# Four graph-attention layers on one core: layer 0 by lists for half of its targets, and masks stored beside the features

## Chip, core and metric

The kernel runs on one core of a Trainium2 chip. TensorE multiplies, VectorE (DVE), ScalarE (ACT) and GpSimd (POOL) compute beside it, and DMA queues of SyncE (SP), ACT and POOL move data between HBM and the on-chip memory. The metric is the time of one execution on the device in microseconds, as the median of several runs.

## What is computed

Four layers of graph attention over 4096 nodes with 256 features. The adjacency is random, and its density falls with the node number, for targets and sources alike: node 0 has most neighbours, node 4095 fewest.

```python
h = relu(layernorm(x))                 # before every layer
# layers 0, 1: g = h @ W; s = g @ a1, t = g @ a2
e = leaky_relu(s[:, None] + t[None, :], 0.2)
p = softmax(where(adj > 0, e, -big), axis=1)
x = x + p @ g                          # layer 0
x = x + elu(p @ g)                     # layer 1
# layer 2: four heads of 64 features, joined; x = x + joined
# layer 3: two softmaxes, of e and of -e, each times a wide projection; x = x + elu(...)
```

## The kernel before

**Tiles.** The 4096 nodes are 32 tiles of 128 (`NT`), or eight blocks of four tiles (`IB` = 512 nodes). Sources are also taken in chunks of four tiles (`CH`); adjT, the transposed adjacency, is read as 64 chunks of 512 sources by 512 targets in int32 (1 MB, two raw tiles of 512 KB each), turned into bytes on VectorE (L1226), and written to HBM as `mask_t`, one tensor per block.

**Weights of the attention.** The exponential of a leaky ReLU is rewritten so that one VectorE instruction, `weigh` (L963), makes the weights of a source tile against one target tile (128x128) or a whole block (128x512): a maximum of a target row and a per-source scalar, times the mask. TensorE multiplies them with the source's features and a column of ones (L999, 128x257; in layer 2 L1024), accumulating over sources in PSUM.

**Two ways to treat targets.** A *dense* unit handles a block of four target tiles against all 32 source tiles: 32 steps of four matmuls. A *listed* unit handles one target tile. The first four source tiles (`DP` = 4), which are dense in the adjacency, are taken from the on-chip memory (`pre`, masks in `mpre`). Of all other sources only those with an edge into the tile are used: their row numbers stand in `idx`, up to 128 in a column, `CAPS[T]` columns for tile T (from 12 for tile 4 down to 6 for the last eight; 218 columns for tiles 4 to 31). For each column an indirect DMA on POOL fetches 128 rows of features from the layer's `table` in HBM (L1320), and the masks of those rows stand in `mlist`, fetched once for all layers by another indirect DMA (L858).

**Stages.** Layer 0 is dense for all eight blocks, and its features `g0` stay on chip. While it runs, `list_sources` makes the lists of blocks 1 to 7: VectorE and TensorE turn the columns of seen edges into positions, build one-hot matrices (`first`, L839, one buffer of 128 x 128 x 28) and multiply them out (L845), then POOL fetches the masks (L858). Layers 1 to 3 are dense for block 0 and listed for tiles 4 to 31, the dense steps (source order 0, 1, 2, ...) spread between the listed tiles.

**Order of the work.** Python generators stand in two queues, `posts` (ends of tiles and rows of the next layer, `node_rows`: layer norm, transpose L691, projection L713, table write L701 on SP) and `lists_q` (lists). `run` walks through a plan of steps and, after each, takes some of the queued work (`rates`). A step is fetched six places ahead of its matmuls, weighed three ahead (`LEAD`). From that program order a scheduler then sets the order of each engine's instructions, POOL's too. The weights of layers 2 and 3 are loaded on ACT's queue and multiplied out between layers 0 and 1, and the rows of the bias are added to x on POOL (L681).

**Buffers.** Four raw tiles, eight weight tiles (`s_work`), nine gathered tiles of features, six PSUM banks for accumulators and two for all else.

Of the kernel before, what the change touches and what calls it, by code (L numbers as in the profile page):

```python
# [451 lines left out]

DP = CH
JT = NT - DP
TS0 = IT
CAPS = (25, 17, 15, 13, 12, 11, 11, 10, 10, 9, 9, 9, 8, 8, 8, 8) + (8,) + (7,) * 7 + (6,) * 8
# [6 lines left out]
GW = tuple(h * p for h, p in zip(LH, PART))  # L463
LEAD = (0, 2, 3, 6)
# [3 lines left out]
def list_layers(ctx: ExitStack, tc: tile.TileContext, a: dict, out: bass.AP, flag):  # L468
# [5 lines left out]
    work = ctx.enter_context(tc.tile_pool(name="s_work", bufs=8))  # L474
# [32 lines left out]
    mask_t = [dram.tile([N + 1, IB], U8, name=f"mask_t{b}", tag=f"mask_t{b}") for b in range(NIB)]  # L507
    table = [None] + [dram.tile([N + 1, GW[l]], F32, name=f"table{l}", tag=f"table{l}") for l in (1, 2, 3)]

    def table_rows(t, jt):  # L510

        r0 = jt // CH * CH * P
        r0 += 1 if r0 >= HALF else 0
        return t[r0 : r0 + CH * P, :].rearrange("(p k) d -> p k d", k=CH)

# [5 lines left out]
    def weights(l, pool, prep, q):  # L521
# [14 lines left out]
        next(L.making)  # L536
# [121 lines left out]
    def node_rows(L, T0):  # L658
# [16 lines left out]
        for k, T in enumerate(tiles):  # L675
            z = rows.tile([P, D], F32, name=f"s_z_{u}_{k}", tag="z", bufs=4)
            nc.vector.tensor_scalar(z, x[:, T, :], mv[:, k, 0:1], 0.0, op0=ALU.subtract, op1=ALU.max)  # L677
            zs.append(z)
# [18 lines left out]
        for k, T in enumerate(tiles):  # L697
            g = L.rows(T)
            yield from project(L, T, g, hTs[k], r[:, 2, k : k + 1])
            if L.table is not None:  # L700
                nc.sync.dma_start(table_rows(L.table, T)[:, T % CH, :], g)  # L701
            L.ready[T] = True

# [48 lines left out]
    def list_constants(pool):  # L752

        place = pool.tile([P, P, JT], F16, name="place")
        nc.gpsimd.iota(
            place, pattern=[[1, P], [0, JT]], base=0, channel_multiplier=0, allow_small_or_imprecise_dtypes=True
# [27 lines left out]
    def list_sources(ib, seen, pool, consts):  # L784

        n = JT * IT
        place, lists, code, sums = consts
        used = pool.tile([P, JT, IT], F16, name=f"used_{ib}", tag="used")
        nc.vector.tensor_scalar(used, seen, 0.0, None, op0=ALU.is_gt)
        yield  # L790
# [43 lines left out]
        yield  # L834
        for t in range(IT):
            T = ib * IT + t
            cap = CAPS[T]
            first = pool.tile([P, P, JT], F16, name=f"first_{T}", tag="first")
            nc.vector.tensor_tensor(  # L839
                first, place, lof[:, t, :].unsqueeze(1).to_broadcast([P, P, JT]), op=ALU.is_equal  # L840
            )
            ps = ps_mm.tile([P, MAXCAP], F32, name=f"idx_ps_{T}", tag="mm")
            yield
            for j in range(JT):
                nc.tensor.matmul(  # L845
                    ps[:, 0:cap],
                    lhsT=first[:, :, j],
# [9 lines left out]
            for k in range(cap):  # L857
# [3 lines left out]
                    in_=mask_t[ib],  # L861
                    in_offset=bass.IndirectOffsetOnAxis(ap=idx[:, k : k + 1], axis=0),
                    element_offset=t * P,
                )
            yield

    index = {}
# [16 lines left out]
    def target_rows(L, T0, nt, big, nact):  # L884
# [3 lines left out]
        grow = (L.big if big else rows).tile(  # L888
            [P, L.H, w], F32, name=f"s_grow_{L.l}_{T0}", tag="growb" if big else "grow"
# [21 lines left out]
    class Unit:  # L911
# [4 lines left out]
        def __init__(u, L, T0, nt, n, get, big=False, heads=None, like=None, cost=1.7, nact=0, rates=(2, 1), per=1):  # L916
# [65 lines left out]
        def multiply(u, i):  # L982
            L, n = u.L, u.L.part - 1
            heads, g, p = u.steps.pop(i)
            first, last = i < u.per, i >= u.n - u.per
# [136 lines left out]
    def run(plan):  # L1122

        n = len(plan)
        for p in range(n + LEAD[3]):
# [5 lines left out]
            if p >= LEAD[3]:  # L1131
# [3 lines left out]
                pump(lists_q, u.rates[1])  # L1135


    with ExitStack() as phase:
# [4 lines left out]
        gpool = phase.enter_context(tc.tile_pool(name="s_g0", bufs=1))  # L1143

# [9 lines left out]
        def zero_rows():  # L1154
# [3 lines left out]
            for b in range(NIB):  # L1158
                nc.sync.dma_start(mask_t[b][HALF : HALF + 1, :], zero[:, 0 : IB // 4].bitcast(U8))
            for l in (1, 2, 3):  # L1160
                for k in range(0, GW[l], D + 2):
                    n = min(D + 2, GW[l] - k)
# [3 lines left out]
        g0 = gpool.tile([P, NT, GW[0]], F32, name="g0")  # L1166
        L0.rows = lambda T: g0[:, T, :]

        def rows_of(L):
            def f(T):  # L1170
                if T < DP:
                    return L.pre[:, T, :]
                return rows.tile([P, GW[L.l]], F32, name=f"s_g_{L.l}_{T}", tag="gout", bufs=3)

            return f

        half = CH // 2

        loaded = {}

        def load(n):

            ib, c = divmod(n, NCH)
            loaded[n] = []
            for h in range(2):
# [8 lines left out]
                loaded[n].append(raw)  # L1194

        def behind(c):
# [5 lines left out]
            if c == 5:  # L1202
                L1 = weights(1, const, prep, nc.sync)
                L1.pre = keep.tile([P, DP, GW[1]], F32, name="pre1")
                L1.rows = rows_of(L1)
                push(posts, L1.making)

        def block(ib):
            masks = {}
            seen = lists_p.tile([P, JT, IT], F32, name=f"seen_{ib}", tag="seen", bufs=2)  # L1210

            def get(jt):
                if jt % CH == 0:
                    c = jt // CH
                    n = ib * NCH + c
                    if n + 1 < NIB * NCH:
                        load(n + 1)
                    if ib == 0:
                        behind(c)
                    m = (  # L1220
                        mpre[:, :, ib * IB : (ib + 1) * IB]
                        if c == 0
                        else mpool.tile([P, CH, IB], U8, name=f"s_m_{ib}_{c}", tag="m")
                    )
                    for h, raw in enumerate(loaded.pop(n)):
# [195 lines left out]
```

## Time and profile before

| | us |
|---|---|
| median of 3 runs (1837.76 to 1842.36) | 1838.87 |
| the profiled execution | 1842.63 |
| its span, first to last instruction | 1840.9 |

| engine | busy us | share of the span |
|---|---|---|
| TensorE matmuls (PE) | 1751.7 | 95% |
| TensorE weight loads (PEld, overlapping) | 1479.2 | 80% |
| VectorE | 1362.7 | 74% |
| POOL | 990.1 | 54% |
| ACT | 607.2 | 33% |

A float32 matmul appears as two records of each kind. Spans on POOL are rough. A share of busy time is an average over four layers that wait for different things, so the stretches have to be read one by one.

### The profile page before, as it was taken

The numbers are of one execution on the slowest core, as the hardware profiler recorded it, in microseconds if no ns is written. First come the engines' busy times: TensorE is split into PE (matmuls) and PEld (weight loads), VectorE is DVE, ScalarE is ACT, GpSimd is POOL, SyncE is SP. The second block draws the span as 40 slices with busy tenths as digits, with TensorE's granted clock in tenths as the row PEclk, the third lists the DMA queues.
The fourth block names the chain that finished last, engine by engine and source line by source line (L and its number), as shares of the span: only waits on it lengthen the run. The fifth ranks groups of instructions, "written<-read, shape, count | busy, mean of one in ns | idle before, by whom it ended". The sixth has DMA issues, their size and how long they took to land.

```text
span 1840.9 us, 29987 instructions
## 1 busy us (share of the span) xinstructions
PE 1751.7 (95%) x9818; PEld 1479.2 (80%) x9818; DVE 1362.7 (74%) x3899; ACT 607.2 (33%) x1793; POOL 990.1 (54%) x950
## 2 busy tenths in 40 slices
PE   6999999999998888988899999999999999999997
PEld 5888888888887666766647777779999888888886
DVE  7766887887884445676689888989888466677775
ACT  5620110110010001233227766769997101111111
POOL 4200677644733767777735555355563477565551
PEclk9999999999999699998999999999999999999999
DMA  7644646635622334454423233333332567656652
GB/s 257 235 154 143 196 121 182 208 108 176 214 58 63 79 108 134 133 152 123 117 66 104 75 93 106 82 91 103 104 94 76 158 204 210 194 171 184 185 153 88
DMA packets 128434, 253.30 MB, mean 138 GB/s; under 512 B 21857, under 2 KB 50958, under 8 KB 128270
## 3 DMA queue, kind: packets, MB, share of 16 engines
q0 software_dynamic: 45344, 119.48, 24.9%
q1 hardware_dynamic: 79690, 129.96, 21.2%
q10 hardware_dynamic: 3236, 1.84, 0.4%
q8 instruction: 81, 1.33, 0.3%
q14 instruction: 83, 0.68, 0.1%
HBM read 215.32 MB, written 35.89 MB: 136 GB/s over the span
## 4 chain that ended last, share of the span: by engine, by line
PE 86%; DVE 5%; DMA 4%; issue 2%; ACT 1%; POOL 1%; ACTq 0%; DVEq 0%; POOLq 0%
PE s_acc L999 51%; PE s_accm L1024 21%; PE s_pj L713 7%; DMA s_gg<-table,idx 4%; PE idx_ps L845 3%; DVE s_p L963 2%; PE s_tp L691 1%; PE s_sT L897 1%; POOL s_gg L1320 1%; DMA s_av<-in_L_av 1%; DVE first L839 1%; PE s_oT L1086 0%; DVE s_z L677 0%; DVE s_st L668 0%; DVE x L1053 0%
## 5 line engine op out<-in xcount | busy, mean ns | idle before, releaser
L1320 POOL DMA_INDIRECT s_gg<-table,idx x654 | 689.4, 1054 | 491.3 <-PE s_acc L999 187.7
L963 DVE SCALAR_TENSOR_TENSOR s_p<-s_grow,s_gg,mlist 128x128 f32<-128x128 f32 x1090 | 344.7, 345 | 187.3 <-DMA s_gg<-table,idx 115.4
L999 PE MATMUL s_acc<-g,s_p 128*128 128x257 f32 x2048 | 463.5, 381 | 0.0
L999 PEld LDWEIGHTS s_acc<-g,s_p 128*128 128x128 f32 x2048 | 383.8, 190 | 51.3
L858 POOL DMA_INDIRECT mlist<-mask_t,idx x218 | 264.8, 1215 | 279.1 <-DVE idx L855 194.8
L999 PE MATMUL s_acc<-s_gg,s_p 128*128 128x257 f32 x1308 | 308.2, 384 | 16.7 <-DVE s_p L963 16.5
L999 PEld LDWEIGHTS s_acc<-s_gg,s_p 128*128 128x128 f32 x1308 | 244.0, 190 | 61.8 <-DVE s_p L963 28.3
L963 DVE SCALAR_TENSOR_TENSOR s_p<-s_grow,g,s_m 128x512 f32<-128x512 f32 x224 | 166.8, 750 | 78.9 <-PE s_acc L999 63.4
L963 DVE SCALAR_TENSOR_TENSOR s_p<-s_grow,pre,mpre 128x128 f32<-128x128 f32 (+1 forms) x588 | 190.2, 364 | 41.0 <-PE s_acc L999 27.1
L1024 PE MATMUL s_accm<-s_p,s_gg 128*65 128x128 f32 x1744 | 202.5, 273 | 0.0
L1024 PEld LDWEIGHTS s_accm<-s_p,s_gg 128*65 128x65 f32 x1744 | 192.6, 138 | 1.9
L949 ACT ACTIVATE s_p<-s_grow,s_minus,s_gg 128x128 f32<-128x128 f32 x436 | 187.0, 486 | 19.4 <-DMA s_gg<-table,idx 7.5
L999 PE MATMUL s_acc<-pre,s_p 128*128 128x257 f32 x768 | 187.7, 388 | 0.9 <-ACT s_y L1110 0.5
L903 ACT ACTIVATE s_grow<-s_sT 128x256 f32<-128x256 f32 (+2 forms) x127 | 45.1, 381 | 410.3 <-PE s_sT L897 360.1
L963 DVE SCALAR_TENSOR_TENSOR s_p<-s_grow,s_gs,s_ms 128x512 f32<-128x512 f32 x196 | 142.6, 746 | 38.6 <-PE s_accm L1024 17.6
L713 PE MATMUL s_pj<-s_w,s_hT 128*128 128x259 f32 (+3 forms) x640 | 167.2, 404 | 2.9 <-ACT s_g L748 2.3
L999 PEld LDWEIGHTS s_acc<-pre,s_p 128*128 128x128 f32 x768 | 146.1, 195 | 24.0 <-DVE s_p L963 0.9
L999 PE MATMUL s_acc<-s_gs,s_p 128*128 128x257 f32 x672 | 157.3, 387 | 0.2 <-DVE s_p L963 0.2
L999 PEld LDWEIGHTS s_acc<-s_gs,s_p 128*128 128x128 f32 x672 | 129.0, 193 | 21.6 <-DVE s_p L963 3.1
L713 PEld LDWEIGHTS s_pj<-s_w,s_hT 128*128 128x128 f32 x640 | 123.6, 201 | 27.2 <-ACT s_g L748 3.4
L1024 PE MATMUL s_accm<-s_p,pre 128*65 128x128 f32 (+1 forms) x928 | 120.6, 284 | 0.0
L1024 PEld LDWEIGHTS s_accm<-s_p,pre 128*65 128x65 f32 x928 | 104.1, 138 | 17.8 <-issue 14.0
(122 smaller groups left out, 1617.6 us busy)
## 6 DMA issues: line engine op xcount, KB each, us to landing
s_raw<-in_adjT SPq DMA_DIRECT2D x128, 512.0 KB
mask_t<-s_m SPq DMA_DIRECT2D x56, 256.0 KB
s_gs<-table SPq DMA_DIRECT2D x21, 516.0 KB
s_gg<-table,idx POOLq DMA_INDIRECT x654, 3.5
table<-s_g SPq DMA_DIRECT2D x28, 258.0 KB
s_ms<-mask_t SPq DMA_DIRECT2D x28, 256.0 KB
x<-in_x SPq DMA_DIRECT2D x8, 512.0 KB
out<-s_out SPq DMA_DIRECT2D x32, 128.0 KB
```

Source lines behind the costliest of these rows:

```text
L691: nc.tensor.transpose(tp[:, c, :], zs[k][:, c * P : (c + 1) * P], ident)
L713: nc.tensor.matmul(ps, lhsT=hT[:, c, :], rhs=L.w[:, c, k * (D + 6) : k * (D + 6) + cols], start=(c == 0), stop=(c == 1),)
L839: nc.vector.tensor_tensor(first, place, lof[:, t, :].unsqueeze(1).to_broadcast([P, P, JT]), op=ALU.is_equal)
L845: nc.tensor.matmul(ps[:, 0:cap], lhsT=first[:, :, j], rhs=val[:, 0:cap, j * IT + t], start=(j == 0), stop=(j == JT - 1),)
L858: nc.gpsimd.indirect_dma_start(out=mlist[:, OFFS[T] + k, :], out_offset=None, in_=mask_t[ib], in_offset=bass.IndirectOffsetOnAxis(ap=idx[: ...
L897: nc.tensor.transpose(ps[:, h - h0, it, :], L.s[:, T0 + it, h : h + 1].to_broadcast([P, P]), ident)
L903: nc.scalar.activation(grow[:, h1:h2, :], ps[:, h1 - h0 : h2 - h0].rearrange("p h a b -> p h (a b)"), AF.Exp, scale=scale,)
L949: nc.scalar.activation(w[:, h, :], u.grow[:, h, :], AF.Relu, scale=g[h][:, n - 1 : n], bias=minus)
L963: nc.vector.scalar_tensor_tensor(p[:, k, :], u.grow[:, h, :], g[k][:, n - 1 : n], m, op0=ALU.min if L.l == 3 and h == 1 else ALU.max, op1= ...
L999: nc.tensor.matmul(u.accs[it][h], lhsT=p[:, k, it * P : (it + 1) * P], rhs=g[k][:, 0:n], start=first, stop=last,)
L1024: nc.tensor.matmul(u.regions[h], lhsT=g[k][:, 0 : DH + 1], rhs=p[:, k, :],  start=first and (u.nt > 1 or h == 0), stop=last, skip_group_ch ...
L1320: nc.gpsimd.indirect_dma_start(out=g, out_offset=None, in_=L.table, in_offset=bass.IndirectOffsetOnAxis(ap=index[T][:, k : k + 1], axis=0),)
```

## The change

1. **Layer 0** is dense for its first four blocks only (`DENSE[0]` = 4). Tiles 16 to 31 become listed units: 64 steps from `g0` and 105 gathered ones. For this layer 0 gets a `table` too, written once per chunk. Masks of blocks 4 to 7 are made by the way: chunk k of these 32 is converted at dense step 2 + 3k (`sides`). From dense step 40 on, one or two listed steps follow each dense one.
2. **Layer 1** is dense for two blocks (`DENSE[1]` = 2); tiles 8 to 31 are listed.
3. **Masks of blocks 1 to 3** have no `mask_t` of their own. They stand as 512 bytes beside the features in the rows of table 2 (block 1) and of table 1 (block 2 ahead of them, block 3 behind). A gather of the first layer that needs them fetches features and mask together, and ACT copies the mask to `mlist` for the later layers. `gather_masks` fetches only those of tiles 16 to 31 (105 instead of 218), one per dense step.
4. **POOL keeps program order** (`manual_schedule`), and makes the normalised rows of layer 0 (`s_z`) in VectorE's place.
5. **Order:** listed tiles run from 16 to 31 and then 8 to 15 in layer 1, from 8 to 31 and then 4 to 7 in layers 2 and 3, and `ORDER` turns the source chunks of the dense units to match; in layer 1 the dense steps are spread over 24 tiles.
6. **Smaller:** one-hots in two buffers of half size, the next made ahead; seven weight tiles instead of eight; weights of layers 2 and 3 on SP's queue and as queued work; delays in `list_sources`; a pool of seven gathered tiles for layer 0.

```diff
+DENSE = (4, 2, 1, 1)
+ORDER = (None, (0, 4, 1, 5, 2, 6, 3, 7), (0, 4, 5, 6, 7, 2, 1, 3), (0, 2, 3, 4, 5, 6, 7, 1))
+LISTED0 = 40
+MW = IB // 4
+MASKS_IN = {1: (2, False), 2: (1, False), 3: (1, True)}
+FRONT = tuple(MW * ((l, False) in MASKS_IN.values()) for l in range(4))
+TW = tuple(FRONT[l] + GW[l] + MW * ((l, True) in MASKS_IN.values()) for l in range(4))
...
-    work = ctx.enter_context(tc.tile_pool(name="s_work", bufs=8))
+    work = ctx.enter_context(tc.tile_pool(name="s_work", bufs=7))
...
+    def mask_rows(b, jt):
+        if b not in MASKS_IN:
+            return table_rows(mask_t[b], jt)
+        l, behind = MASKS_IN[b]
+        c0 = FRONT[l] + GW[l] if behind else 0
+        return table_rows(table[l], jt)[:, :, c0 : c0 + MW].bitcast(U8)
...
-            nc.vector.tensor_scalar(z, x[:, T, :], mv[:, k, 0:1], 0.0, op0=ALU.subtract, op1=ALU.max)
+            (nc.gpsimd if L.l == 0 else nc.vector).tensor_scalar(z, x[:, T, :], mv[:, k, 0:1], 0.0, op0=ALU.subtract, op1=ALU.max)
...
-            if L.table is not None:
-                nc.sync.dma_start(table_rows(L.table, T)[:, T % CH, :], g)
             L.ready[T] = True
+            if L.l == 0 and T % CH == CH - 1:
+                nc.sync.dma_start(feature_rows(L.l, T), L.g[:, T - CH + 1 : T + 1, :])
+            elif L.l > 0:
+                nc.sync.dma_start(feature_rows(L.l, T)[:, T % CH, :], g)
...
+        def one_hot(T, j):
+            first = pool.tile([P, P, half], F16, name=f"first_{T}_{j}", tag="first", bufs=2)
...
+    def gather_masks(n, tile=None):
+        for T, k in list(masks_of):
+            if not n or tile is None and T not in index:
+                break
+            if tile in (None, T):
                 nc.gpsimd.indirect_dma_start(
                     out=mlist[:, OFFS[T] + k, :],
...
+            if (L.l, u.T0, i) in copies:
+                nc.scalar.copy(*copies.pop((L.l, u.T0, i)))
...
+    def listed_sources(L, T, pool):
...
+                at, behind = MASKS_IN.get(T // IT, (0, False))
+                own = at == L.l > 0
+                if at == 0:
+                    gather_masks(CAPS[T], T)
+                more = 0 if not own else (T % IT + 1 if behind else IT - T % IT) * MW // IT
+                wide = pool.tile([P, GW[L.l] + more], F32, name=f"s_gg_{L.l}_{T}_{k}", tag="gg")
...
+                if own:
+                    c0 = (GW[L.l] + more) * 4 - P if behind else 0
+                    kept, m = m, wide.bitcast(U8)[:, c0 : c0 + P]
+                    copies[L.l, T, i] = kept, m
...
+        dense_steps = DENSE[0] * NT
+        sides = [2 + 3 * k for k in range((NIB - DENSE[0]) * NCH)]
...
-        run([s for ib in range(NIB) for s in block(ib).plan()])
+        plan, listed = [], []
+        for T in range(DENSE[0] * IT, NT):
+            u = Unit(L0, T, 1, DP + CAPS[T], listed_sources(L0, T, gat0), cost=0.45, rates=(1, 2, 0))
+            listed += u.plan()
+        for ib in range(DENSE[0]):
+            for step in block(ib).plan():
+                plan.append(step)
+                if ib * NT + step[1] >= LISTED0:
+                    n = 1 + step[1] % 2
+                    plan += listed[:n]
+                    del listed[:n]
+        run(plan + listed)
...
-        L = weights(l, late, prep, nc.scalar)
+        L = weights(l, late, late, nc.sync)
...
+    push(posts, late_weights())
...
+        tail = DENSE[0] if l == 1 else DENSE[1]
+        for T in (*range(tail * IT, NT), *range(DENSE[l] * IT, tail * IT)):
...
-        alone, over_tiles = ((0, 0), (16, 14), (36, 14), (16, 28))[l]
+        alone, over_tiles = ((0, 0), (16, 24), (36, 14), (16, 28))[l]
...
-        list_layers(tc, a, out, flag)
+        with tc.manual_schedule(engines={mybir.EngineType.Pool}):
+            list_layers(tc, a, out, flag)
```

## The prediction

> **What bounds the kernel now.** First the head of the page. Its second number is the share of the span.
>
> ```profile
> span 1840.9 us, 29987 instructions
> ...
> PE 1751.7 (95%) x9818; PEld 1479.2 (80%) x9818; DVE 1362.7 (74%) x3899; ACT 607.2 (33%) x1793; POOL 990.1 (54%) x950
> ```
>
> TensorE looks full, but an average over four layers hides what each one waits for. So I cut the span where the layers change: the first and last starts of the matmuls, listed by tile, give 586 us for the last layer-0 matmul, 625 for the first of layer 1, 937 and 1421 for the next two. Then I ask for busy time by stretch (columns: stretch, its length, PE, PEld, DVE, ACT, POOL, granted clock, DMA share, GB/s).
>
> ```profile
> 0.00:586.00 586.00, 571.73 (x3148) 495.86 (x3148) 443.73 (x959) 112.60 (x402) 272.95 (x272) 1.00 0.52 162
> 586.00:625.00 39.00, 22.78 (x172) 18.99 (x171) 19.10 (x67) 7.32 (x27) 20.93 (x18) 0.60 0.39 109
> 625.00:937.00 312.00, 267.37 (x1140) 213.16 (x1140) 185.60 (x627) 68.63 (x242) 222.84 (x225) 0.94 0.45 124
> 937.00:1240.00 303.00, 300.36 (x1958) 225.82 (x1957) 270.43 (x785) 197.64 (x510) 150.70 (x134) 1.00 0.32 88
> 1240.00:1421.00 181.00, 180.48 (x1491) 170.21 (x1490) 161.31 (x577) 167.81 (x474) 94.52 (x84) 1.00 0.34 96
> 1421.00:1840.90 419.90, 409.01 (x1916) 355.13 (x1914) 282.55 (x889) 53.24 (x139) 228.13 (x218) 0.99 0.58 170
> ```
>
> Layer 0 (0 to 586) is TensorE's own work: only 14 us idle, nearly all in the first 30 us. Then 39 us in which TensorE does little. Layer 1 (to 937) is not TensorE's: POOL counts 223 of 312 us busy and has 0.30 us between gathers on top. Layers 2 and 3 are TensorE's again, with ACT nearly as full in 1240 to 1421. The waits of layer 1 alone (waiter, released by: us, times, longest) say the same:
>
> ```profile
> DVE s_p L963 <- DMA s_gg<-table,idx: 79.4, 84, 2.3
> POOL s_gg L1320 <- PE s_acc L999: 35.8, 78, 9.7
> ```
>
> VectorE waits for gathered rows; POOL itself rarely waits. A gather takes it 0.99 us there plus the 0.30, so 1.29, and 218 of them fill 281 of the 312 us. The unit costs come from the groups of the page and of layer 0 (busy, mean ns) and from the timeline (start, duration):
>
> ```profile
> L1320 POOL DMA_INDIRECT s_gg<-table,idx x654 | 689.4, 1054 | 491.3 <-PE s_acc L999 187.7
> L963 DVE SCALAR_TENSOR_TENSOR s_p<-s_grow,s_gg,mlist 128x128 f32<-128x128 f32 x1090 | 344.7, 345 | 187.3 <-DMA s_gg<-table,idx 115.4
> L963 DVE SCALAR_TENSOR_TENSOR s_p<-s_grow,g,s_m 128x512 f32<-128x512 f32 x224 | 166.8, 750 | 78.9 <-PE s_acc L999 63.4
> L1226 DVE TENSOR_SCALAR s_m<-s_raw 128x1024 uint8<-128x1024 int32 x112 | 78.7, 717 | 5.7 <-DMA s_raw<-in_adjT 4.9
> ```
>
> ```profile
> 555.67 30.30 PE L999 MATMUL s_acc<-g,s_p 128*128 128x257 f32 x139
> 568.80 1.43 POOL L858 DMA_INDIRECT mlist<-mask_t,idx  x1 [0.30 <-issue]
> ...
> 616.81 0.95 POOL L858 DMA_INDIRECT mlist<-mask_t,idx  x1 [0.30 <-issue]
> ```
>
> A matmul of 128x257 is two records here: 30.30 / 139 = 0.218 us a record, 0.436 us a matmul, 1.744 us a dense step of four.
>
> **What the Trainium skill says.** "SBUF — State Buffer", section "SBUF: two separate sides": VectorE and GpSimd share a port pair under an exclusive lock, and a GpSimd DMA cannot write its descriptors while VectorE holds it. The trace agrees in direction: the same gather repeats every 1.73 us beside the 512-wide L963 and every 1.25 us once that has stopped. "DMA: Bandwidth & Descriptors", section "Specifications": about 358 GB/s of HBM for a core, and pieces of 512 B or more for full rate. No stretch here shows 358 held; layer 0's slices of 15 us top out at 293 GB/s, so I use 293. "TensorE: Matmul & The Clock Gate", section "What's actually happening": an idle array falls to a lower clock. The trace agrees: 0.60 in the 39 us gap and 0.94 in layer 1, 1.00 in layer 0.
>
> **The change, part by part.**
>
> *Layer 0, TensorE.* Four dense blocks go: 4 x 32 x 4 = 512 matmuls. Tiles 16 to 31 come instead with 4 + CAPS steps each: 64 + 105 = 169. So 343 matmuls fewer, 343 x 0.436 = 149.5 us, all in the stage that TensorE bounds. The lists of the last block (4 tiles x 1.95 us of matmuls by the timeline) and four more rows of layer 1 (85 us of L713 and L691 for 60 tiles, 1.4 each) now fall inside it, with 12 more transposed rows: +15. TensorE alone would end layer 0 at 586 - 149.5 + 15 = 451 us.
>
> *What must now fit beside it.* VectorE: 443.7 - 128 x 0.750 (dense weights) + 169 x 0.345 - 32 x 0.37 (the s_z of layer 0, moved to POOL) + 17 (last list, four rows) = 411 us, 91% of 451 against 76% before. POOL: 105 mask gathers and 105 new feature gathers, none possible before tile 16 starts, which in the order of the changed kernel's instructions is dense step 41. Up to there TensorE needs 15 us of start, 41 x 1.744, 36 row tiles x 1.4 and three lists, about 143 us. 210 gathers at 1.52 (layer 0's mean of 1.22 plus 0.30) take 319 us, so POOL would end at 462; at 1.73 it would be 506. The 32 s_z and 32 additions, some 0.88 each by L681, are done before. DMA: all 64 chunks of adjT are read in the first 96 steps instead of 256. Of these 56 come by step 95, with their masks 1.31 MB each, 73 MB; with x, the new table 0, first rows of table 1 and half of the gathers about 92 MB. At 293 GB/s that is 314 us; TensorE needs 315 to there (15 + 96 x 1.744 + 82 listed x 0.436 + 47 row tiles x 1.4 + 16 list tiles x 1.95). Only four raw tiles (two chunks) are in flight. Three engines and the DMA within 10% of each other never overlap fully: I take +36, so 487. Bounds: 0 (451) and +75 (POOL's slow pitch and the raw stream in turn).
>
> *Gap 586 to 625.* It held the last list, the last rows and the weights of layers 2 and 3, loaded and multiplied in a row. Now the last list runs under 37 listed steps left after the dense ones, and the weights are background work. 39 becomes 5; bounds 0 and 20. What is late next: tile 31's row must reach the table before layer 1's first gather, some 15 us, covered by 16 dense steps alone (28 us).
>
> *Layer 1.* Two dense blocks instead of one: +128 matmuls, tiles 8 to 31 instead of 4 to 31: 330 - 270 = 60 fewer, so +68, +29.6 us of TensorE. 44 gathers fewer: 174 x 1.29 = 224 us of POOL, plus 18 of start, is 242. TensorE before, by rows: 458 x 0.436 + 34 (L713) + 12 (L691) + 10 (L897) = 256; after, 285. So TensorE now comes last: 285 + 5 = 290 against 312. Bounds: 275 (busy overcounts short records) and 312 (POOL's wider rows as slow as the time saved). 69 gathers bring 128 to 512 B of mask in the same row; a gather's issue is by row, so I take nothing more, up to 69 x 0.1. Their 69 copies to mlist are ACT's, idle 243 of 312 us: nothing; without that cover, 69 x 0.28 = 19.
>
> *Layers 2 and 3.* Same matmuls, tile order turned so that block 1 comes last. 44 copies of about 0.28 (nearest row: ACT's 128x128, 0.275) land in 1240 to 1421, where ACT has 13 us left of 181: half shows, +6, bounds 0 and +14. So 490. Layer 3: 420 as before, within 5. ORDER follows the turned tiles; one work buffer fewer (7) leaves VectorE's lead of three steps; both nothing. s_z, halved one-hots (56 of half size for 28), zero rows, and mask rows of 512-B pieces: nothing, VectorE's and SP's slack covers them; without it some 10 us of DMA. POOL in program order: its L1320 waits for TensorE in layer 1 (35.8 us) come from a late buffer, not from the order; +-10.
>
> Sum: 487 + 5 + 290 + 490 + 420 = **1692 us of span**. The profiled execution took 1842.63 with a span of 1840.9, so 1.7 around it; the median of the runs, 1838.87, lies 3.8 below that execution. 1692 + 1.7 - 3.8 = 1690.
>
> **Rivals.**
> *Everything hides:* 451 + 0 + 275 + 484 + 416 = 1626, with one or two stalls 1640. For it: before, TensorE in layer 0 waited for nothing. Against: VectorE at 91%.
> *POOL or the raw stream bounds layer 0:* it ends at 530 to 560, so 1735 to 1765. For it: 1.73 us a gather, two chunks of lookahead. Against: before, VectorE hardly waited for raws (4.9 us in all at the L1226 group above).
> *Slower: SP's queue holds the raws back.* SP is in order, and some 28 row writes of tables 0 and 1 stand between the raws and wait for ACT:
>
> ```profile
> SPq L701 <- ACT s_g L748: 326.2, 49, 40.5
> ```
>
> That is 6.7 us a wait. If each of 28 kept the raws back by that, layer 0 gains 186 us and the total is 1876. It decides from 149 / 28 = 5.3 us each. Against: before, the raws behind these waits had no free buffer anyway.
> That the change would not do what it says is small here: the dropped matmuls stand in the instruction order; only layer 1 staying POOL's (312, total 1712) is inside the range.
>
> **Numbers.** Forecast as it stands, 1660 to 1720: 0.65. All hidden, below 1660: 0.10. Layer 0 bound by POOL or raws, 1720 to 1790: 0.19. SP's queue, at or above the old time: 0.05, and 0.01 for about no change. Less than 0.3% is what a measurement of this kernel cannot tell from no change. So faster 0.94, same 0.01, slower 0.05. Leaving out 2 in 10 gives 1640 to 1765.
>
> **What would show it.** Right: layer 1's first matmul near 490, TensorE above 90% from 60 us on in layer 0, POOL no longer VectorE's first releaser in layer 1, about 1840 - 150 in all. Wrong: VectorE waiting for s_raw or s_gg in layer 0 by tens of us (second rival), L1306 waiting for ACT before raws (third), or layer 2 longer by more than 15 us, which no step here explains.

## The result, and the profile after

The changed kernel took 1696.87 us (median of 4 runs, 1695.88 to 1698.29) against 1840.61 for the kernel before (4 runs): a ratio of 0.922, 95% interval 0.9203 to 0.9238. The forecast was 1690, range 1640 to 1765. Its profiled execution took 1697.57 us, 1.8 around a span of 1695.8.

The head of the page after, to be laid beside the one before:

```profile
span 1695.8 us, 29208 instructions
...
PE 1619.6 (96%) x9268; PEld 1366.4 (81%) x9268; DVE 1321.9 (78%) x3908; ACT 632.6 (37%) x1915; POOL 959.8 (57%) x930
```

TensorE lost 132 us of work and its share rose by one point. Where the 145 us of span went is read from the first and last matmuls of each layer's own tiles (s_acc, s_accm, listed by tile):

| stage | before | forecast | after |
|---|---|---|---|
| start to layer 1's first matmul | 625.1 | 492 | 487.7 |
| of it behind layer 0's last | 39 | 5 | 5.3 |
| layer 1 | 310.8 | 290 | 295.4 |
| layer 2 | 485.5 | 490 | 493.4 |
| layer 3 and the end | 419.5 | 420 | 419.3 |

Busy time by stretch of the kernel after (columns as in the prediction):

```profile
0.00:482.00 482.00, 444.08 (x2586) 372.57 (x2586) 404.20 (x1037) 117.61 (x426) 329.46 (x320) 0.99 0.76 234
482.00:487.30 5.30, 3.09 (x15) 2.15 (x15) 4.11 (x17) 1.73 (x5) 0.00 (x0) 0.82 0.66 199
487.30:640.00 152.70, 152.40 (x730) 131.78 (x729) 104.72 (x324) 36.27 (x129) 91.74 (x92) 0.99 0.52 148
640.00:783.00 143.00, 124.36 (x553) 104.18 (x552) 84.09 (x254) 45.00 (x163) 81.05 (x83) 0.93 0.49 140
783.00:1080.00 297.00, 297.00 (x1874) 217.98 (x1872) 266.62 (x782) 196.66 (x516) 134.52 (x121) 1.00 0.33 89
1080.00:1280.00 200.00, 194.05 (x1626) 185.78 (x1625) 173.60 (x614) 182.80 (x539) 105.15 (x97) 1.00 0.37 103
1280.00:1695.80 415.80, 404.66 (x1896) 351.97 (x1894) 284.52 (x885) 52.57 (x138) 217.87 (x218) 0.99 0.59 172
```

Layer 0 is still nearly TensorE's: 38 us idle, 15 of them in the first 120. The gap is gone. Layer 1 has two parts: TensorE is full to 640 us, and idle for 18.6 of the 143 us behind that. There, from 664 us on, the listed tiles are 8 to 15, whose gathers bring a mask and whose copies run on ScalarE. The groups that answer to those shown before, and s_z in layer 0:

```profile
L1231 POOL DMA_INDIRECT s_gg<-table,idx x715 | 751.7, 1051 | 643.8 <-PE s_acc L1071 219.4
L1033 DVE SCALAR_TENSOR_TENSOR s_p<-s_grow,s_gg,mlist 128x128 f32<-128x128 f32 x994 | 316.3, 349 | 103.1 <-PE s_acc L1071 55.3
L929 POOL DMA_INDIRECT mlist<-mask_t,idx x105 | 123.9, 1180 | 61.8 <-issue 29.1
L702 POOL TENSOR_SCALAR s_z<-x,s_mv 128x256 f32<-128x256 f32 x32 | 46.4, 1460 | 7.3 <-PE s_tp L716 6.1 <-DVE s_m L1325 1.2
```

Unit prices are as before (gathers 1.05, weights of 128 columns 0.35); 113 gathers of masks are gone, and those that remain last 1.18, near the 1.22 taken. The waits of layer 1, 487 to 783 us:

```profile
POOL s_gg L1231 <- PE s_acc L1071: 61.7, 69, 12.9
ACT mlist L1056 <- DMA s_gg<-table,idx: 59.6, 55, 3.4
DVE s_r L709 <- ACT s_r L698: 17.9, 9, 6.1
DVE s_p L1033 <- DMA s_gg<-table,idx: 15.7, 12, 2.4
```

VectorE waits 15.7 us for gathered rows where it waited 79.4, and POOL waits 61.7 us for TensorE where it waited 35.8. A new waiter stands near the top: ScalarE, whose copies of masks (L1056) wait for the same gathers and have row work behind them in order. TensorE's idle time from 640 to 783 us is nearly all in four waits for row work, the steps that turn a finished tile into a row of the next layer (s_r, s_tp, s_hT); POOL waits for TensorE there too:

```profile
PE s_sT L967 <- ACT s_hT L718: 7.8, 2, 5.3
PE s_tp L716 <- DVE s_r L709: 4.9, 1, 4.9
PE s_tp L716 <- DVE s_r L711: 4.6, 1, 4.6
...
POOL s_gg L1231 <- PE s_acc L1071: 29.7, 28, 4.0
```

The timeline at 728 us shows one of the four:

```profile
733.10 0.30 ACT L1056 COPY mlist<-s_gg 128x128 uint8<-128x128 uint8 x1 [1.00 <-DMA s_gg<-table,idx]
...
733.87 0.20 ACT L698 ACTIVATE s_r<-s_r 128x2 f32<-128x2 f32 x1
...
734.10 0.16 DVE L709 SCALAR_TENSOR_TENSOR s_r<-s_mv,s_r 128x2 f32<-128x2 f32 x1 [4.61 <-ACT s_r L698]
...
734.29 0.69 PE L716 MATMUL s_tp<-s_ident,s_z 128*128 128x128 f32 x2 [4.88 <-DVE s_r L709]
```

So there were two questions for experiments: what keeps layer 0 at 482 where TensorE alone was put at 451, and whether these copies cost layer 1 its 18.6 us.

### The profile page after: what moved, and what is told of

Read it like the earlier page. It is cut to its first block, busy times and chain, and to the rows that moved or that the text cites. A ratio compares the mean times of both kernels' runs of the same rounds, so it can differ in the third digit from the quotient of the medians.

```text
span 1695.8 us, 29208 instructions
## 1 busy us (share of the span) xinstructions
PE 1619.6 (96%) x9268; PEld 1366.4 (81%) x9268; DVE 1321.9 (78%) x3908; ACT 632.6 (37%) x1915; POOL 959.8 (57%) x930
## 4 chain that ended last, share of the span: by engine, by line
PE 52%; DMA 2%; DVE 1%; ACT 1%; issue 0%; POOL 0%; ACTq 0%; DVEq 0%; POOLq 0%
PE s_acc L1071 24%; PE s_accm L1096 22%; PE s_pj L748 3%; DMA s_gg<-table,idx 2%; PE s_sT L967 1%; PE s_tp L716 1%; PE s_oT L1158 0%; ACT s_p L1019 0%; DVE s_p L1033 0%; ACT mlist L1056 0%; DMA out<-s_out 0%; DVE s_p L1042 0%; POOL s_gg L1231 0%; DVE s_y L1187 0%; DVE s_out L1138 0%
## 5 line engine op out<-in xcount | busy, mean ns | idle before, releaser
L1231 POOL DMA_INDIRECT s_gg<-table,idx x715 | 751.7, 1051 | 643.8 <-PE s_acc L1071 219.4
L1033 DVE SCALAR_TENSOR_TENSOR s_p<-s_grow,s_gg,mlist 128x128 f32<-128x128 f32 x994 | 316.3, 349 | 103.1 <-PE s_acc L1071 55.3
L1071 PE MATMUL s_acc<-s_gg,s_p 128*128 128x257 f32 x1430 | 348.1, 387 | 6.3 <-DVE s_p L1033 6.3
L1071 PEld LDWEIGHTS s_acc<-s_gg,s_p 128*128 128x128 f32 x1430 | 268.0, 192 | 47.9 <-DVE s_p L1033 11.5
L1071 PE MATMUL s_acc<-g,s_p 128*128 128x257 f32 x1152 | 283.4, 387 | 13.2 <-DVE s_p L1033 9.1
L1071 PEld LDWEIGHTS s_acc<-g,s_p 128*128 128x128 f32 x1152 | 214.0, 192 | 46.9 <-DVE s_p L1033 14.7
L1071 PE MATMUL s_acc<-s_gs,s_p 128*128 128x257 f32 x896 | 203.7, 380 | 0.0
L1071 PEld LDWEIGHTS s_acc<-s_gs,s_p 128*128 128x128 f32 x896 | 169.4, 190 | 25.1 <-DVE s_p L1033 1.1
L973 ACT ACTIVATE s_grow<-s_sT 128x256 f32<-128x256 f32 (+2 forms) x136 | 46.7, 367 | 346.9 <-PE s_sT L967 310.8
L929 POOL DMA_INDIRECT mlist<-mask_t,idx x105 | 123.9, 1180 | 61.8 <-issue 29.1
L1019 ACT ACTIVATE s_p<-s_grow,s_minus,pre 128x128 f32<-128x128 f32 x224 | 96.4, 487 | 19.1 <-issue 11.6
```

The costliest lines, as they stand in the source:

```text
L929: nc.gpsimd.indirect_dma_start(out=mlist[:, OFFS[T] + k, :], out_offset=None, in_=mask_t[T // IT], in_offset=bass.IndirectOffsetOnAxis(ap= ...
L973: nc.scalar.activation(grow[:, h1:h2, :], ps[:, h1 - h0 : h2 - h0].rearrange("p h a b -> p h (a b)"), AF.Exp, scale=scale,)
L1019: nc.scalar.activation(w[:, h, :], u.grow[:, h, :], AF.Relu, scale=g[h][:, n - 1 : n], bias=minus)
L1033: nc.vector.scalar_tensor_tensor(p[:, k, :], u.grow[:, h, :], g[k][:, n - 1 : n], m, op0=ALU.min if L.l == 3 and h == 1 else ALU.max, op1= ...
L1071: nc.tensor.matmul(u.accs[it][h], lhsT=p[:, k, it * P : (it + 1) * P], rhs=g[k][:, 0:n], start=first, stop=last,)
L1231: nc.gpsimd.indirect_dma_start(out=wide, out_offset=None, in_=L.table, in_offset=bass.IndirectOffsetOnAxis(ap=index[T][:, k : k + 1], axis=0),
```

## The experiments

When the experiments ran, the kernel before took 1990 to 1994 us and the changed one 1785, with the same durations of single instructions, so each experiment is compared with the kernels run at that time and not with the 1840 and 1697 above. All stages are cut at the same matmuls; the ratio is to the kernel before, run in turn with each. "To layer 1" runs to layer 1's first matmul and so takes in the gap behind layer 0's last. Three things limit the comparisons. The stages are those of one execution each; c_after's was the fastest of its four (1776.3 to 1799.2), e6's the slowest of its four (1814.6 to 1836.7). Kernels with no reason to differ begin layer 1 anywhere from 516.4 to 522.7 (c_after, e1, e3), and their later stages differ by up to 10, so less than 10 us in a stage is not read as an effect. And e9, e8, e6 and e12 ran on another chip than c_after, where the kernel before took 1990 us against 1994, so for them the ratios count beside the medians; on which chip the first runs were is not known.

| kernel | median us | ratio (95%) | to layer 1 | layer 1 | layer 2 | rest |
|---|---|---|---|---|---|---|
| changed (c_after) | 1785.3 | 0.8977 (0.8908-0.9046) | 516.4 | 313.3 | 517.4 | 427.5 |
| e1, copies on VectorE | 1787.5 | 0.9062 (0.8925-0.9199) | 522.7 | 306.7 | 518.6 | 432.2 |
| e1 again | 1788.8 | 0.8985 (0.8925-0.9046) | 518.2 | 316.7 | 518.7 | 426.9 |
| e3, half the raws | 1783.8 | 0.9060 (0.8902-0.9217) | 520.0 | 311.6 | 514.8 | 429.8 |
| e2, conversions on ScalarE | 1786.6 | 0.8966 (0.8906-0.9026) | 526.8 | 310.2 | 517.0 | 428.8 |
| e4, no mask gathers | 1734.0 | 0.8790 (0.8658-0.8923) | 482.6 | 309.3 | 514.5 | 426.3 |
| e4 again | 1738.0 | 0.8729 (0.8671-0.8788) | 478.6 | 310.6 | 520.6 | 424.2 |
| e11, five dense blocks | 1814.9 | 0.9189 (0.9041-0.9337) | 534.6 | 335.5 | 520.3 | 423.5 |
| e9, layer 0 dense | 1909.4 | 0.9623 (0.9544-0.9702) | 619.9 | 343.3 | 513.9 | 429.6 |
| e8, masks apart | 1923.9 | 0.9647 (0.9585-0.9709) | 608.9 | 372.3 | 514.4 | 429.7 |
| e6, POOL scheduled | 1822.4 | 0.9136 (0.9080-0.9192) | 568.0 | 315.6 | 520.6 | 430.8 |
| e12, masks in table 0 | 1795.6 | 0.9014 (0.8962-0.9067) | 536.7 | 313.0 | 517.7 | 427.9 |

**The measure: the changed kernel itself.**

> The changed kernel itself, unaltered, as the measure for the kernels that run beside it: in the runs before, its layer 0 could be read only from its first profile, and the kernel before took 1992 us on that occasion against 1840 in its first runs. If the occasion is like the first: 1697 us and a ratio of 0.922; if like the last: 1780 to 1790 us and a ratio of 0.895 to 0.91.

It gained more than at first: 209 us, not 144. Its layers 0 and 2 are where the trace differs most: 29 us more to layer 1 and 24 in layer 2 than in the first profile. PE, DVE and ACT wait 91 us in all, until layer 1's start, for what the profile calls "issue" or "remote", that is, for no release that it shows; in the first profile of the same kernel this sum is 0.4. The 91 us count stretches in which several wait at once, and TensorE's own share is 9. Of the 29 us, 13 are matmuls that took longer (460.1 us busy against 447.2, at a mean clock of 0.95) and 16 more idle time of TensorE. Some of the larger waits, by waiter, in that stretch:

```profile
ACT s_grow L973 <- issue: 20.6, 1, 20.6
...
ACT s_hT L718 <- remote: 18.3, 4, 8.0
...
DVE s_p L1033 <- remote: 7.5, 4, 3.9
ACT s_g L770 <- remote: 5.8, 2, 5.4
PE s_acc L1071 <- issue: 4.1, 4, 2.1
```

The timeline at 427 us shows what one looks like:

```profile
423.61 0.75 PE L716 MATMUL s_tp<-s_ident,s_z 128*128 128x128 f32 x4
...
428.17 0.95 POOL L929 DMA_INDIRECT mlist<-mask_t,idx  x1 [0.30 <-issue]
429.07 0.75 DVE L1033 SCALAR_TENSOR_TENSOR s_p<-s_grow,g,s_m 128x512 f32<-128x512 f32 x1 [1.69 <-remote]
429.11 0.37 ACT L718 COPY s_hT<-s_tp 128x256 f32<-128x256 f32 x1 [8.03 <-remote]
429.53 0.99 PEld L748 LDWEIGHTS s_pj<-s_w,s_hT 128*128 128x128 f32 x4 [2.76 <-issue]
```

ScalarE could have copied s_tp at 424.4, when its transposes were done. It starts at 429.1, within 0.1 us of VectorE, which had stood since 427.4, while POOL issued gathers throughout. TensorE goes on 0.4 us later; its next matmul reads the s_hT that this copy makes, so its own wait may be no more than that. What holds ScalarE and VectorE is not in the trace.

**The copies of masks on VectorE (e1, run twice).**

```diff
 # multiply
-            if (L.l, u.T0, i) in copies:
-                nc.scalar.copy(*copies.pop((L.l, u.T0, i)))
 # weigh, at its end
+            if (L.l, u.T0, i) in copies:
+                nc.vector.tensor_copy(*copies.pop((L.l, u.T0, i)))
```

> The changed kernel with one move: the 113 copies of a gathered row's mask into mlist are VectorE's (issued in weigh, behind the operation that waits for the same gather), not ScalarE's (issued in multiply). Theory, ScalarE's in-order queue: in 640 to 783 us of the changed kernel ScalarE's copies waited 59.6 us for gathers and TensorE did 124.4 of 143 us; with the copies elsewhere some two thirds of those 18.6 us come back, and a few of layer 2's 6 us of TensorE idle in 1080 to 1280: layer 1 ends 10 to 13 us after its start earlier, and the total is 1680 to 1687 us. Rival, late gathers hold TensorE there whoever copies: 1694 to 1699. A second rival, 113 more operations on VectorE cost more than they free: above 1700.

> Again the changed kernel with the 113 copies of a mask on VectorE instead of ScalarE, now beside the changed kernel itself. Theory, ScalarE's in-order queue costs TensorE's idle time at the end of layer 1: 10 to 17 us below the changed kernel beside it. Rival, late gathers hold TensorE whoever copies: within 3 us of it.

No gain: 1787.5 and 1788.8 beside 1785.3, layer 1 at 306.7 and 316.7 around 313.3. But the wait moved with the copy, as the waits of layer 1 show, of the changed kernel and of the second run:

```profile
ACT mlist L1056 <- DMA s_gg<-table,idx: 58.9, 52, 3.4
```

```profile
DVE mlist L1052 <- DMA s_gg<-table,idx: 38.3, 38, 2.7
```

The copies did not stay behind the weights that wait for the same gather, as my expectation has it. The scheduler put them ahead of weights and of row work, here at 753 us of the second run:

```profile
753.65 0.23 DVE L1052 COPY mlist<-s_gg 128x128 uint8<-128x128 uint8 x1 [1.98 <-DMA s_gg<-table,idx]
753.79 0.58 DVE L702 TENSOR_SCALAR s_z<-x,s_mv 128x256 f32<-128x256 f32 x1
755.73 0.23 DVE L1052 COPY mlist<-s_gg 128x128 uint8<-128x128 uint8 x1 [1.36 <-DMA s_gg<-table,idx]
755.87 0.15 DVE L709 SCALAR_TENSOR_TENSOR s_r<-s_mv,s_r 128x2 f32<-128x2 f32 x1
```

So the chain at 728 us was not taken away but moved to another queue in order, and moving it is worth nothing. What the copies cost layer 1 where they stand is not shown: no run has layer 1 without them and nothing else changed.

**Half of the side blocks' raw reads left out (e3).**

```diff
+                if DROP.get(ib, {}).get(c) == h:      # one half in 7 of 8 chunks of blocks 4 to 7
+                    loaded[ib, c].append(None)        # not read; its mask is written as zeros
+                    continue
```

> The changed kernel without half of the raw reads of blocks 4 to 7: for 7 of the 8 chunks of each of these blocks one half (512 KB of adjT) is not read, and its mask is written as zeros by an operation of the same size on VectorE, so VectorE, POOL and TensorE keep their work and DMA loses 28 x 0.52 = 14.7 MB of the 95.9 MB of the first 340 us. Left out: the edges of those half chunks. Theory A, the raw stream sets the 31 us by which layer 0 outlasts TensorE's own 451: layer 0 ends at 450 to 462, total 1665 to 1678. Theory B, VectorE's 404 us of work sets it: layer 0 stays at 478 to 482, total 1692 to 1697.

DMA lost 14.7 MB, VectorE's wait for raws fell from 13.9 to 6.1 us, and layer 1 began at 520.0; the two kernels with the same layer 0 as the changed one and all raws (e1) began it at 522.7 and 518.2. On that occasion the raw stream doesn't set the end of layer 0. Its layer 0 has 91 us of the waits without a release as well, so this doesn't exclude the raws for the first profile, where they made VectorE wait 15.7 us.

**Half of the conversions on ScalarE (e2).**

```diff
+                if ib > 0 and h == 1:
+                    nc.scalar.copy(m[:, h * half : (h + 1) * half, :], raw)
+                else:
                     nc.vector.tensor_scalar(m[:, h * half : ...], raw, 0.0, None, op0=ALU.is_gt)
```

> The changed kernel with half of the conversions of raw adjacency to masks (every second one of blocks 1 to 7, 56 of 128x1024) on ScalarE as a copy of the 0s and 1s, instead of VectorE: VectorE loses 56 x 0.72 = 40 us of its 404 in layer 0, ScalarE gets some 56 x 1.0. Theory B, VectorE sets layer 0's excess of 31 us: layer 0 ends 20 to 30 us earlier than beside. Theories A and C: within 5 us. Rival below nothing: the copies wait for raws in ScalarE's queue and hold back the row tiles' transposes behind them: layer 0 up to 20 us longer.

VectorE's work up to layer 1 fell from 408.75 (the changed kernel, first row below) to 373.38 us. The stage is 10 us longer in the profiled executions, but the medians are 1786.6 and 1785.3, so I read neither gain nor loss.

```profile
0.00:516.40 516.40, 460.12 (x2600) 383.06 (x2601) 408.75 (x1054) 119.78 (x431) 325.44 (x320) 0.95 0.72 220
```

```profile
0.00:526.80 526.80, 464.28 (x2600) 385.93 (x2601) 373.38 (x998) 173.12 (x487) 307.50 (x320) 0.94 0.70 215
```

Of the rival that I put below nothing, its mechanism is there: ScalarE's conversions wait for raws in its queue (59.6 us, 15 times, longest 11.6). So VectorE's load isn't excluded as a cause by this run; it only shows that 35 us less of it did not help in this form.

**No mask gathers in layer 0 (e4, run twice).**

```diff
-                m = mlist[:, OFFS[T] + k, :]
+                m = mlist[:, OFFS[T] + k, :] if at else onesm
-                if at == 0:
-                    gather_masks(CAPS[T], T)
 # run
-                gather_masks(u.rates[2])
```

> The changed kernel without the 105 mask gathers of tiles 16 to 31: in all layers their masks are one constant tile of ones of the same size and type (left out: the masks of these tiles), so POOL loses 105 x (1.18 + 0.30) = 155 us in layer 0 and DMA 105 x 16 KB; the other engines keep their work. Theory C, POOL sets the 31 us: layer 0 ends at 450 to 465, total 1665 to 1680. Theories A and B (raw stream, VectorE): at most 5 us[...]: 1690 to 1697.

> Again the changed kernel without the 105 mask gathers of layer 0 (left out: the masks of tiles 16 to 31, a tile of ones in their place), now beside the changed kernel itself. Theory C, POOL's 155 us of gathers set what layer 0 takes beyond TensorE's work: its layer 0 ends 20 to 35 us earlier than that of the changed kernel beside it. Theories A and B: at most 5 us earlier. A first run of it ended layer 0 at 478 us, where a kernel with the changed kernel's own layer 0 ended at 520 on the same occasion, so if that was no chance, some 40 us or, at the quicker gathers of the first profile, 5.

This is the one that moves layer 0: its layer 1 begins 37.8 us earlier than that of the changed kernel beside it, the total is 47 us lower, and the waits without a release fall from 91 us to 7.

```profile
0.00:478.60 478.60, 444.68 (x2601) 374.94 (x2602) 404.71 (x1054) 119.61 (x431) 211.68 (x216) 0.99 0.75 234
```

TensorE, VectorE, clock and DMA rate are those of the first profile after (444.08, 404.20, 0.99, 234). So on that occasion the mask gathers held layer 0. POOL's 155 us alone need not be the reason: the waits that went with them show no release, and the gathers' transfers went too. In the first profile layer 1 began at 487.7; if this kernel's 478.6 would have been the same then, which was not run, the gathers cost some 9 us there.

**All masks by gathers of their own (e8).**

```diff
-MASKS_IN = {1: (2, False), 2: (1, False), 3: (1, True)}
+MASKS_IN = {}
 # masks_of: all tiles from 4 on, 218 gathers
```

> The changed kernel with no masks in the tables' rows: all 218 listed steps of tiles 4 to 31 get their mask by a gather of its own (113 more on POOL, 113 x 1.48 = 167 us, in layer 0 and at layer 1's start), and no copies. Theory, POOL and its gathers are the dear thing beside the dense steps: 40 to 110 us slower than the changed kernel. Rival, mask gathers hide beside TensorE's work: within 10 us of it, either sign, since ScalarE loses 113 copies and the feature gathers are narrower.

139 us slower (133 by the ratios): 92.5 in the stage to layer 1 with 62 more mask gathers there, 59 in layer 1 with 51 more, -3 in layer 2. The waits without a release in layer 0 are 229 us. The gathers of layer 1 by group, in its stretch:

```profile
L930 POOL DMA_INDIRECT mlist<-mask_t,idx x51 | 49.3, 967 | 15.5 <-issue 14.6 <-DMA mlist<-mask_t,idx 0.9
```

51 gathers of 0.97 + 0.30 us are 65 us of POOL, and layer 1 got 59 us longer: hardly any of it was hidden. Which way they cost it isn't shown. POOL is busy for 223.9 of the 372.3 us, and the waits without a release of PE, DVE and ACT in layer 1 rise from 36 us in the changed kernel to 171.

**Layer 0 dense again (e9), and five dense blocks (e11).**

```diff
-DENSE = (4, 2, 1, 1)
+DENSE = (8, 2, 1, 1)          # e11: (5, 2, 1, 1)
-        tail = DENSE[0] if l == 1 else DENSE[1]
+        tail = 4 if l == 1 else DENSE[1]
 # masks_of: tiles 16 to 31, as before
```

> The changed kernel with its main part undone: all eight blocks of layer 0 dense (DENSE[0] = 8, no listed tiles in layer 0), the rest as changed: GpSimd in program order, masks of blocks 1 to 3 in the tables' rows, halved one-hots, two dense blocks in layer 1, layers 2 and 3 as changed. Theory: the swap alone moved layer 0 from 586 to 482, so this kernel is 104 us (and up to 149.5, the price of the 343 matmuls, if mask gathers cost the changed layer 0 more on this occasion) slower than the changed one, and 40 to 50 us faster than the kernel before: layer 1's 16 and the gap's 30 remain. Rival, the swap brought less and the masks in the rows more: within 80 us of the changed kernel.

> The changed kernel with block 4 of layer 0 dense again (five dense blocks, tiles 20 to 31 listed; layers 1 to 3 as they are): 128 matmuls for 4 x 4 + 29 = 45, so 83 more, 36 us of TensorE; VectorE gets 32 x 0.750 - 45 x 0.345 = 8.5 us more, POOL 29 gathers of features fewer in layer 0, and the raws of layer 0 have 128 dense steps instead of 96. If TensorE alone set layer 0: total 1733. If the raw stream or POOL set it, part of the 36 us is hidden: 1705 to 1720. If VectorE sets it: about 8 us more, 1703 to 1708.

e9 takes the swap of layer 0 back and keeps the rest: the stage to layer 1 is 103.5 us longer, and TensorE's busy time in it 593.47, 133.4 us more (149.5 - 15 = 134.5 was the forecast's working).

```profile
0.00:619.90 619.90, 593.47 (x3292) 509.45 (x3292) 456.89 (x1012) 120.48 (x428) 171.23 (x193) 0.98 0.53 163
```

That the stage agrees with the 104 expected is partly luck, for those were layer 0 alone: up to the last matmul of layer 0 it is 89 us longer (599.6 against 510.8), and the other 15 are the gap behind it. e9 ends 80 us below the kernel before, where I expected 40 to 50 from the first runs. And I missed layer 1 in it: 30 us longer, with 24 mask gathers that were not issued before the last list and fell into layer 1.

e11 has 21 of them there, and its layer 1 is 22.2 us longer. Its layer 0 hides all 36 us of added matmuls, with 84 mask gathers in the stage instead of 105: the last one starts at 511.4, against 510.8. What makes the stage 18.2 us longer is the gap behind it, shown here (granted clock 0.70):

```profile
511.80:534.60 22.80, 17.40 (x143) 14.12 (x141) 12.27 (x42) 7.21 (x26) 11.40 (x10) 0.70 0.29 70
```

In both kernels no listed steps are left behind the dense ones, and the last lists, which stand in that gap, have nothing to run under: it is 20.3 and 23.2 us, against 5.6 in c_after. With e8 these are three kernels in which a gather added to layer 1 goes with 1.06 to 1.25 us, nearly its full pitch. The waits without a release in layer 1 rise with them too, from 36 to 77 (e11), 87 (e9) and 171 us (e8), so POOL's pace is not shown to be the way.

**GpSimd left to the scheduler (e6).**

```diff
-        with tc.manual_schedule(engines={mybir.EngineType.Pool}):
-            list_layers(tc, a, out, flag)
+        list_layers(tc, a, out, flag)
```

> The changed kernel with GpSimd's instructions left to the scheduler instead of in program order. Theory (the prediction's): the order itself is worth nothing, within 10 us. Rival: in program order the masks' gathers stand one by one between the features' gathers; where the scheduler bunches them, tiles wait for features and layer 0 or 1 is 15 to 40 us longer.

The median is 37 us higher, and by the ratios, whose intervals don't meet, it is 32 us. The stage to layer 1 is 51.6 longer in the profiled execution, its slowest, and the waits without a release there are 161 us. So the order was worth something then; since those waits hide what each engine waits for, how the order acts stays open.

**A version meant to be better (e12).**

```diff
-MASKS_IN = {1: (2, False), 2: (1, False), 3: (1, True)}
+MASKS_IN = {1: (2, False), 2: (1, False), 3: (1, True), 4: (0, False), 5: (0, True)}
-        sides = [2 + 3 * k for k in range((NIB - DENSE[0]) * NCH)]
+        sides = [1 + 5 * k // 2 if k < 16 else 41 + 3 * (k - 16) for k in ...]
-                own = at == L.l > 0
+                own = at == L.l
 # work buffers: 5 in layer 0, 7 behind it
```

> A version meant to beat the changed kernel: masks of blocks 4 and 5 lie in table 0's rows (before and behind the features), so that the gather of a feature brings its mask and 57 of the 105 mask gathers of layer 0 go; the side chunks of blocks 4 and 5 come every 2.5 dense steps so that they are written by step 40, those of 6 and 7 every 3 from 41; layer 0 has 5 work buffers. The run without any mask gathers was 47 us faster than the changed kernel beside it. Theory C (POOL's gathers): 57/105 of that, 20 to 30 us below the changed kernel. Rival: denser raws early, wider gathered rows and 57 copies on ScalarE eat it: within 5 us.

It brought no gain: the median is 10 us higher, with ratios that overlap, and the stage to layer 1 is 20.3 longer than in c_after's fastest execution, though the waits without a release fell to 41 us. Waits of that stage:

```profile
ACT mlist L1057 <- DMA s_gg<-table,idx: 140.8, 52, 13.7
...
DVE s_m L1327 <- DMA s_raw<-in_adjT: 24.0, 17, 4.4
...
DVE s_r L709 <- ACT s_r L698: 14.0, 5, 6.3
```

Several things changed at once, and which of them ate the gain is open. Copies wait up to 13.7 us each in ScalarE's queue, ahead of the row tiles that fill table 1. The denser raws make VectorE wait (24.0 against 13.9 us), and TensorE does 96.8 us of work in the first 120 where it did 104.6. The first gather of features comes at 168.6 us instead of 138.1, behind one POOL wait of 59.9. Five work buffers instead of seven were not tried alone. No complete version beats the changed kernel; e4, which does, leaves masks out.

## Why the prediction was right, step by step

**TensorE's share of layer 0: right.** 343 matmuls for 149.5 us less 15 was the largest term. e9 measures 133.4 us of busy time, and 103.5 of the stage, on the later occasion. Against the 447.2 us that the changed kernel was busy up to there in its first profile, it would be 146.

**"Three engines and the DMA within 10% of each other never overlap fully: I take +36": right size (+31), mechanism only in part.** I left open which of them it would be. TensorE's own work was 444 busy plus 15 of start, 8 more than my 451. The 23 us left are what my 36 stood for. Of their causes, e3 speaks against the raw stream on the later occasion. The DMA ceiling of 293 GB/s that I took from the trace was a wrong reading: before, the 15 us from 5 to 20 show 367 GB/s and those from 285 to 300 show 303; after, 83 to 98 us shows 379. So the about 358 that the Trainium skill, "DMA: Bandwidth & Descriptors", section "Specifications", has for a core's HBM was no ceiling here either. The mask gathers are what layer 0 is sensitive to, by 37.8 us in e4; in the first profile by that comparison, which was not run, some 9. Many short waits stand beside that: TensorE waits 14.3 us for s_p and its weight loads, beside it, 23.4, none over 2.3. Whether a less busy VectorE would shorten them e2 didn't settle.

**The gap, 39 to 5: right** (5.3). The last list runs under listed steps and the late weights in the background. e9 and e11, which have no listed steps left there, show gaps of 20.3 and 23.2 us; the weights were not tried alone.

**Layer 1, 290: near (295.4), in part by luck.** I had 285 us of TensorE's work and 5 idle; it was 276.8 and 18.9, and the two errors nearly cancel. "TensorE now comes last" holds to 640 us, where it is busy 152.4 of 152.7. The term that was mis-sized is the idle time behind that: 18.6 us, 17.2 of them in four waits for row work of 2.4 to 5.3 us, shown above. POOL isn't simply the pace there: its 83 gathers take 81.05 + 83 x 0.30 = 106 us, less than TensorE's 124, and it waits 29.7 us for TensorE to free a gathered tile. My sum over the whole layer, 242 us of POOL against 285, says nothing about the small steps that finish a tile. What makes the row work late is open. The chain through ScalarE's copies was seen and not taken away, so "69 copies on ScalarE: nothing" is not settled; that ScalarE has idle time is no cover by itself, as the lines at 728 us show, where its queue holds rows back. Against the copies as the only cause speaks the kernel before, which has none and yet five waits of TensorE for ScalarE's s_r, of 2.3 to 3.7 us each, from 858 to 927 us. The second dense block of layer 1 was not tried alone.

**Layers 2 and 3: right in size, wrong in the reason for layer 2.** It took 8 us more where 6 was taken, and I put the 6 down to copies in a full ScalarE. The trace splits the 8 otherwise: TensorE's busy time in the layer rose by 5.0 us (482.24 to 487.25) and its idle time by 2.8. The busy part is row work that now falls behind layer 2's first matmul, before and after:

```profile
L713 PE MATMUL s_pj<-s_w,s_hT 128*128 128x268 f32 x8 | 2.0, 389 | 0.0
```

```profile
L748 PE MATMUL s_pj<-s_w,s_hT 128*128 128x268 f32 x24 | 5.9, 389 | 0.0
```

So at most 2.8 of the 8 can be the copies'. e1 and e8 move layer 2 by +1.3 and -3.0, less than two runs of one kernel differ (e4: 514.5 and 520.6).

**"POOL in program order: +-10": too narrow.** On the occasion of the experiments it was worth 32 to 37 us (e6).

**What I left out: fewer mask gathers are themselves a gain.** The change takes 113 of them off POOL. I counted that only as relief for layer 0, where 105 features' gathers take their place. e8 puts them back: 139 us. It and e9 (124 us) can't be added, since both leave mask gathers over for layer 1 (51 and 24), and their sum is more than the whole gain of 209. The larger gain on the second occasion fits this: the kernel before issues 218 of them and lost 154 us against its first runs, the changed one with 105 lost 88. It isn't shown, since there is no trace of the kernel before from that occasion; and in its first profile, with 194 of them in layer 0, TensorE was idle for 14 us.

**The rivals.** *Everything hides* (1640) failed by TensorE's idle time: 38 us in layer 0, 15 of them in the first 120, and 19 in layer 1. *POOL or the raws bound layer 0* did not happen in the first runs, where VectorE waited 15.7 us for raws and 9.0 for gathered rows up to 482 us; the mask gathers did hold it on the later occasion, whichever way they do. *SP's queue holds the raws back* fell: SP did wait for row writes, as its own waits up to 482 us show, but 15 times 3.4 us and 3 times 11.9, not 28 times 6.7, and VectorE found raws 15.7 us late in sum.

```profile
SPq L729 <- ACT s_g L783: 50.5, 15, 12.4
...
SPq L729 <- ACT s_r L697: 35.6, 3, 25.4
```

## What to carry to other kernels

A sum of busy times over a layer hides a stretch in which the fullest engine waits for a chain of small steps: cut the layer where the kind of step changes, and ask in each part what that engine waits for. When a gather brings a row anyway, let it bring the small thing that a second gather would fetch; but ask which in-order queue then has to unpack it, and what stands behind. Before believing a chain of waits seen in a timeline, take it away once, and look in the new trace whether it is gone: here the copies went from ScalarE to VectorE, and the wait and the work behind it went along. And a total that comes out right can hold two errors that cancel: compare each term, busy and idle apart.

## What the runs showed of the hardware

- **On the later occasion, waits that show no release grew with the number of mask gathers.** Until layer 1's start, PE, DVE and ACT together waited so for 7 and 8 us with no mask gathers (e4), 41 with 48 (e12), 56 with 84 (e11), 74 to 107 with 105 (changed, e1, e3, e2), 229 with 167 (e8). In layer 1 it was 26 to 52 with none (36 in the changed kernel), 77 with 21 (e11), 87 with 24 (e9) and 171 with 51 (e8). The number isn't all: e6 has 161 with 105 before layer 1, and e9 only 13 with 81, which come with 2 feature gathers beside them. In the first profiles of the changed kernel and of the one before, with 105 and 194 in layer 0, the sum is 0.4 and 0. What differs between the two occasions, and what the engines wait for, stays open.
- **An elementwise operation was dear on GpSimd, mostly by itself.** s_z, 128x256, took 1.46 us on POOL in the mean, where the same line is about 0.35 on VectorE. Five of the 32 ran with no VectorE operation beside them and took 1.13 to 1.14, so about 0.3 of the 1.1 us goes with a busy VectorE. A mask gather took 1.18 us in layer 0 of the changed kernel and 0.97 in layer 1 of e8. The direction of these two differences is that of the Trainium skill, "SBUF — State Buffer", section "SBUF: two separate sides", on the port pair that the two share. In e2, with 35 us less work on VectorE, the gathers before layer 1 took 1.08 and 1.09 us (masks and features) against 1.17 and 1.14 in the changed kernel beside it; but in e6, with no less, they took 1.07 and 1.12, so it isn't the only thing.
